# A four-layer graph network on gathered neighbours: scores one block ahead of the products, and a norm split over two engines, in layers two and three

## The chip, the cores and the metric

The kernel runs on one core of a Trainium2 chip. The metric is the device time of one execution in microseconds (us), lower is better; a version is stood for by the median of its runs. Five engines with queues of their own work side by side and wait for each other by semaphores: TensorE (PE; PEld is its weight load), VectorE (DVE), ScalarE (ACT), GpSimd (POOL) and SyncE (SP, which only issues transfers here).

## The reference

A graph of 4096 nodes with 256 features each goes through four pre-norm layers. Every layer is `x = x + attention(relu(layernorm(x)), adj)`, and they differ in the attention:

- layers one and three: four heads, score of an edge = leaky ReLU of a term of the node plus a term of its neighbour, softmax over the neighbours, weighted sum of the neighbours' projected rows (layer one has an ELU behind it);
- layer two: the same with one head; the projected row is added, and the unprojected rows are summed;
- layer four: four heads, score = q times k, softmax, weighted sum of v.

The adjacency is drawn with about eight edges to a node, besides a self loop, so a node has at most 23 neighbours here.

## The kernel before

**Tiling.** The nodes are sorted by their number of neighbours and cut into 32 blocks of 128, one node to a partition. `CAPS[b]` is the largest number of neighbours in block b, from 23 down to 3. A layer is 32 steps, one block to a step, in the order `ORDER`: 0, 30, 1, 29, 2, 28 and so on, and last 14, 16, 15, 31. In the code the four layers are l = 0 to 3; layers two and three are l = 1 and l = 2. The stages of the program one after the other: the scan of the adjacency (0 to some 371 us, with part of layer one in it), the rest of layer one (`late`), then `layer(1)`, `layer(2)` and `layer(3)`.

**Rows by gather.** Every layer reads the rows of its neighbours from a table in DRAM that the layer before wrote. One neighbour slot of one block is one indirect DMA of 128 rows, issued by POOL (`fetch`, L1030) into a ring of slots in SBUF: 270 gathers to a layer (a block's own cap, 15 at most, and one for the nodes with more). `fill(i)` puts the gathers of up to four blocks ahead of step i into POOL's queue; the first gather of a block waits for the last product of the blocks that had its slots (L1357). A layer's first gather waits for the whole table.

**A step of layers two and three.** For block b = `ORDER[i]`:

- `scores` (L1495): ACT (l = 1) or DVE (l = 2) adds the neighbours' terms, which waits for the block's gathers; for l = 1 DVE also compares lists (`mutual`, L1564 and L1568, which read the gathers too); DVE takes leaky ReLU and maximum (L1522, L1548 or L1552), ACT the exponential (L1550 or L1556).
- `weigh` (L1571): DVE normalises the shares (L1582 to L1584), multiplies the block's own row (L1595) and the gathered rows (L1610), and PE sums the rows into a PSUM bank (L1590, L1617, L1623). I call these the products of the block.
- `settle` (L1630): DVE adds up the sum into x (L1644) and takes mean and variance (`normed`, L955 and L957); ACT makes scale and bias of it in eight small instructions (L960 to L967).
- `norm`: ACT applies norm and ReLU (L970), PE transposes (L980). `flip`: ACT copies the transposed block to SBUF (L982).
- `product`: PE multiplies with the next layer's weights (L1023). `third`: DVE or ACT moves the result out of PSUM (l = 1: L1663 or L1665; l = 2: four instructions of DVE, L1683 to L1694, and ACT's squares, L1697), and SP writes it to the next layer's table (L1667, L1685). I call this the row of the block.

**Order.** PE, DVE, ACT and SP run their instructions in the order in which the code emits them, and in layers two and three POOL too. The stages of older blocks stand in a step at fixed lags: with `left` steps to go, `settle` is S blocks behind, `norm` N, `flip` F, `product` Q and `third` T. Far from the end these are 2, 3, 4, 5 and 6, and at the end 1, 2, 2, 2 and 3. A step emits `norm`, `product`, `scores`, `weigh`, `settle`, `flip`, `third`. There are four PSUM banks for the transposes and the rows; when none is free, `room` emits older `flip` and `third` stages early. A stage that reads a bank in a later step than the one that filled it waits for the last product of the step that filled it (`told_by`, L1385). PSUM also holds the shares, in two halves that the blocks take in turn (`self.turns`).

Of the kernel before, what the change touches and what calls it, by code (L numbers as in the profile page):

```python
# [9 lines left out]
F32 = mybir.dt.float32  # L10
# [9 lines left out]
P = 128  # L20
D = 256
# [52 lines left out]
RAW = 6  # L74

AHEAD = 4

BOUND = 4900.0


class Sparse:
# [869 lines left out]
    def normed(self, pool, xt, name):  # L951

        nc, act = self.nc, self.nc.scalar.activation
        st = pool.tile([P, 6], F32, name=f"s_st_{name}", tag="st", bufs=3)
        nc.vector.bn_stats(st, xt)  # L955
        mv = pool.tile([P, 2], F32, name=f"s_mv_{name}", tag="mv1", bufs=3)
        nc.vector.bn_aggr(mv, st)  # L957
        y = pool.tile([P, 6], F32, name=f"s_y_{name}", tag="y1", bufs=3)
        log, root, less, minus, r, at = (y[:, k : k + 1] for k in range(6))
        act(log, mv[:, 1:2], AF.Ln, bias=self.eps)  # L960
        act(less, mv[:, 1:2], AF.Identity, bias=self.minus, scale=-0.5)
        act(root, log, AF.Exp, scale=-0.5)
        act(minus, mv[:, 0:1], AF.Copy, scale=-1.0)
        act(log, root, AF.Square)
        act(less, less, AF.Identity, bias=self.three, scale=log)
        act(r, less, AF.Copy, scale=root)
        act(at, minus, AF.Copy, scale=r)  # L967
        yield None
        h = pool.tile([P, D], F32, name=f"s_h_{name}", tag="h", bufs=2)
        act(h, xt, AF.Relu, bias=at, scale=r)  # L970
        yield h

# [337 lines left out]
    def layer(self, l):  # L1310


        nc, nt, vs = self.nc, self.nt, {}
# [65 lines left out]
                held[j] = (s, s + room)  # L1379
                at = s + room if K else at  # L1380

        sums, behind, turning, flipped, rows = {}, {}, {}, {}, {}
        self.spot, signals, when = None, {}, {}

        def told_by(i, others, step):  # L1385
# [11 lines left out]
        def settle(c):  # L1397
            behind[c] = self.settle(l, c, sums.pop(c), made)
            for _ in range(2):
                next(behind[c])  # L1400

        def room(k):
            if len(self.free) < k:
                upto("flip", done["norm"] - 1)
                upto("third", done["product"] - 1)

        def norm(d):
            if l < 3:
                room(1)
                turning[d] = self.turned(self.pool, next(behind.pop(d)), f"{l + 1}_{d}")  # L1410
                next(turning[d])
                when["turn", d] = now, self.wrote

# [29 lines left out]
                self.tc.declare_no_dep(i, group="results", reason="places differ")  # L1443
                self.tc.add_to_no_dep_group("results", i)

        stages = {"settle": settle, "norm": norm, "flip": flip, "product": product, "third": third}
        done = {name: 0 for name in stages}

        def upto(name, k):
            while done[name] <= k:  # L1450
                stages[name](ORDER[done[name]])
                done[name] += 1

        for i in range(nt):
            now = i
            left = nt - 1 - i
            if l == 3:
                S = 1 if left < 3 else 2
                N = F = Q = S + 1
                T = N  # L1460
            else:
                S = 1 if left < 5 else 2
                N = 2 if left < 4 else 3
                Q = 2 if left < 2 else 3 if left < 4 else 4 if left < 6 else 5
                F, T = max(N, Q - 1), Q + 1
            fill(i)
            if (l, i) == (2, 4):
                self.symmetric()
            b = ORDER[i]
            upto("norm", i - N)  # L1470
            upto("product", i - Q)
            g = ring[:, held[b][0] : held[b][1], :]
            p = self.scores(l, b, self.rows[b], g)
            if l == 3:
                upto("third", i - T)
            sums[b] = self.weigh(l, b, vs.pop(b) if l == 3 else self.rows[b][:, 0:D], g, p)
            start, end = held.pop(b)
            past.append((start * wide, end * wide, self.read))
            if l < 3:
                signals[i] = self.read[1]  # L1480
            upto("settle", i - S)
            if l < 3:
                upto("flip", i - F)
                upto("third", i - T)
        now = nt
        upto("norm", nt - 2)
        upto("third", nt - 3)
        upto("product", nt - 2)
        upto("settle", nt - 1)
        upto("norm", nt - 1)  # L1490
        upto("third", nt - 2)
        upto("product", nt - 1)
# [2 lines left out]
    def scores(self, l, b, mine, g):  # L1495

        nc, pool = self.nc, self.pool
        H = 1 if l == 1 else 4
        G = self.slots(l, b)
        K = CAPS[b]  # L1500
        more = b == 0
        e = pool.tile([P, TOPK, H], F32, name=f"s_e_{l}_{b}", tag="e", bufs=3)
        ek = e[:, : K + 1, :].rearrange("p k h -> p (k h)")
        if l < 3:
            src = mine[:, D + H : D + 2 * H]
            if l == 1:
                nc.scalar.activation(e[:, :G, 0], g[:, :G, D], AF.Identity, bias=src)
                nc.scalar.activation(e[:, K, :], mine[:, D : D + H], AF.Identity, bias=src)
            else:
                first = nc.vector.tensor_tensor(e[:, K, :], mine[:, D : D + H], src, ALU.add)  # L1510
                nc.vector.tensor_tensor(
                    e[:, :G, :], g[:, :G, D : D + H],
                    src.unsqueeze(1).to_broadcast([P, G, H]), ALU.add,
                )
            if l == 1:
                self.mutual(b, g)

                nc.scalar.copy(self.near[:, b, 0:G], g[:, :G, WL - 1])
            if more:
                self.more_scores(l, mine, g[:, KEPT, :], e)  # L1520
            slope = 0.01 if l == 1 else 0.2
            steep = nc.vector.scalar_tensor_tensor(ek, ek, slope, ek, ALU.mult, ALU.max)  # L1522
            if l == 2:
                self.tc.declare_no_dep(steep.ins, first.ins, reason="another sum comes after it")
        else:
            q = self.shares[:, IB - D :]
            nc.scalar.copy(q, mine[:, 0:D])
            nc.scalar.copy(e[:, K, :], self.eself[:, b, :])
            for k0 in range(0, G, AT_ONCE):
                m = min(AT_ONCE, G - k0)  # L1530
                kq = g[:, k0 : k0 + m, 0:D]
                nc.vector.tensor_tensor(  # L1532
                    kq, kq, q.unsqueeze(1).to_broadcast([P, m, D]), ALU.mult
                )
                nc.vector.tensor_reduce(  # L1535
                    e[:, k0 : k0 + m, :], kq.rearrange("p k (h d) -> p k h d", h=4), AX.X, ALU.add
                )
            nc.vector.tensor_tensor(
                e[:, :G, :], e[:, :G, :],
                self.away[:, b, :G].unsqueeze(2).to_broadcast([P, G, 4]), ALU.add,  # L1540
            )
            if more:
                self.more_scores(l, mine, g[:, KEPT, :], e)
        by_head = e[:, : K + 1, :].rearrange("p k h -> p h k")
        top = pool.tile([P, H], F32, name=f"s_m_{l}_{b}", tag="m", bufs=3)
        p = self.shares[:, ts(self.turns % 2, TOPK * H)].rearrange("p (k h) -> p k h", h=H)
        if l == 1:
            nc.vector.tensor_reduce(top, by_head, AX.X, ALU.max, negate=True)  # L1548
            tot = pool.tile([P, H], F32, name=f"s_t_{l}_{b}", tag="t", bufs=3)
            nc.scalar.activation(ek, ek, AF.Exp, bias=top, accum_out=tot)  # L1550
            return e, p, tot
        nc.vector.tensor_reduce(top, by_head, AX.X, ALU.max)  # L1552
        nc.vector.tensor_tensor(  # L1553
            by_head, by_head, top.unsqueeze(2).to_broadcast([P, H, K + 1]), ALU.subtract
        )
        nc.scalar.activation(p[:, : K + 1, :].rearrange("p k h -> p (k h)"), ek, AF.Exp)  # L1556
        return p, p, None
# [13 lines left out]
    def weigh(self, l, b, me, g, made):  # L1571
# [12 lines left out]
        nc.vector.tensor_tensor(  # L1584
            whole(p), whole(exps), tot.unsqueeze(2).to_broadcast([P, H, K + 1]), ALU.mult
        )
        self.turns += 1
        v0 = 0 if l < 3 else D
        acc = self.pacc.tile([P, 2, D], F32, tag="acc", name=f"s_acc_{l}_{b}")
        self.took_x[b] = nc.tensor.matmul(  # L1590
# [39 lines left out]
    def settle(self, l, b, acc, made):  # L1630


        nc, pool = self.nc, self.pool
        xt = self.x[b]
        yield None
        if l == 3:
            tag = ("out", "kv")[ORDER.index(b) % 2]
            wide_as = 2 * D if tag == "kv" else D
            y = pool.tile([P, wide_as], F32, name=f"s_out_{b}", tag=tag, bufs=3)[:, 0:D]
            nc.vector.tensor_reduce(y, acc.rearrange("p u d -> p d u"), AX.X, ALU.add)  # L1640
            made.append((self.out, self.own(b), y))
            yield None
            return
        s = nc.vector.tensor_reduce(xt, acc.rearrange("p u d -> p d u"), AX.X, ALU.add)  # L1644
        self.tc.declare_no_dep(
            s.ins, self.took_x.pop(b).ins, reason="the sum's last product comes after it"
        )
        yield from self.normed(pool, xt, f"{l + 1}_{b}")
# [627 lines left out]
```

## Time and profile before

| | |
|---|---|
| runs shown | median 1672.91 us of 9 (1669.1 to 1674.16) |
| the profiled execution | 1673.22 us, its span 1671.5 us |
| busy share of the span | POOL 68%, DVE 66%, PE 65%, ACT 32% |
| mean granted clock of PE | 0.829 |
| layer two's gathers | 542.8 to 880.1 us |
| layer three's gathers | 906.6 to 1244.7 us |
| layer four's gathers and sends | 1279.4 us to the end |

The profile is of one execution. Its busy shares count work alone: POOL's queue also spends some time between two gathers that is not counted. Times of rows below count from the start of the span; the execution is 1.7 us longer than its span.

### The profile page before, as it was taken

To read this page: it belongs to the slowest core of one execution; us is meant where nothing else is said; L and a number is where in the kernel's file an instruction comes from. 1 tells how busy PE (TensorE), PEld (TensorE's weight loads), DVE (VectorE), ACT (ScalarE), POOL (GpSimd) and SP (SyncE) were. 2 spreads that over 40 slices of the span, in tenths; PEclk is the share of its full clock that TensorE was granted. 3 is DMA by queue.
4 is the path that set the end of the run, shared out by engine and by line. 5 is a ranking of instruction groups with operands and counts; after the bars stand their busy time and mean duration, and the time that the engine had idled before them with its cause. 6 is when DMAs were issued, how large, how long until landed. Compare 5 with 4: busy or idle time off the path is not lost.

```text
span 1671.5 us, 14539 instructions
## 1 busy us (share of the span) xinstructions
PE 1081.1 (65%) x3166; PEld 588.0 (35%) x3179; DVE 1109.2 (66%) x2651; ACT 536.1 (32%) x1754; POOL 1140.9 (68%) x1241
## 2 busy tenths in 40 slices
PE   5858888705776357777784467878794464645455
PEld 4423333204443134444342234444452232322232
DVE  6669899816885255455552456766774797888786
ACT  6866664003344033343343023333342000000000
POOL 1267777767774777777772777777752777777775
PEclk9969989856897678898897689999997677777877
DMA  7899999476551444444452435444443776767674
GB/s 271 299 396 394 358 395 325 143 230 161 156 164 64 116 118 129 131 132 132 130 140 63 109 108 145 137 134 139 141 127 97 216 220 205 213 206 211 205 206 130
DMA packets 125910, 309.11 MB, mean 185 GB/s; under 512 B 35028, under 2 KB 53463, under 8 KB 125816
## 3 DMA queue, kind: packets, MB, share of 16 engines
q0 software_dynamic: 66832, 203.64, 41.6%
q1 hardware_dynamic: 58984, 104.46, 17.6%
q8 instruction: 29, 0.48, 0.1%
q14 instruction: 65, 0.53, 0.1%
HBM read 273.00 MB, written 35.00 MB: 184 GB/s over the span
## 4 chain that ended last, share of the span: by engine, by line
POOL 26%; DMA 23%; DVE 20%; issue 16%; ACT 9%; PE 5%; DVEq 0%; SPq 0%; POOLq 0%; ACTq 0%
POOL s_ring L1030 22%; DMA s_ring<-s_tab,s_near 11%; DMA s_raw<-in_adj_dram 11%; DVE s_ring L1610 5%; DVE s_ring L1532 2%; ACT s_low L277 2%; DVE s_e L1535 2%; POOL s_placed L721 2%; PE s_bank L1023 1%; DVE s_rx L1644 1%; DVE s_me L1595 1%; POOL s_g L1030 1%; PE s_acc L1617 1%; PE s_ps_t L1023 1%; POOL out_dram L1047 1%
## 5 line engine op out<-in xcount | busy, mean ns | idle before, releaser
L1030 POOL DMA_INDIRECT s_ring<-s_tab,s_near x900 | 854.4, 949 | 338.0 <-issue 262.7
L1617 PE MATMUL s_acc<-s_ring,s_ident 128*128 128x512 f32 (+1 forms) x1002 | 467.1, 624 | 276.6 <-DVE s_ring L1610 276.4
L1617 PEld LDWEIGHTS s_acc<-s_ring,s_ident 128*128 128x128 f32 x1002 | 226.5, 233 | 494.8 <-DVE s_ring L1610 305.8
L1030 POOL DMA_INDIRECT s_g<-s_tab,s_keep x192 | 182.8, 952 | 129.6 <-DMA s_raw<-in_adj_dram 65.1
L1610 DVE TENSOR_TENSOR s_ring<-s_ring,s_shares 128x2048 f32<-128x2048 f32 (+1 forms) x153 | 233.0, 1553 | 0.0
L277 ACT ACTIVATE s_low<-s_raw 128x1024 fp8e4<-128x1024 int32 x128 | 135.1, 1056 | 61.2 <-DMA s_raw<-in_adj_dram 59.6
L1556 ACT ACTIVATE s_shares<-s_e 128x40 f32<-128x40 f32 (+7 forms) x64 | 13.1, 205 | 329.6 <-DVE s_e L1553 329.6
L520 PE MATMUL s_pt<-s_low,s_mark_True 128*128 128x512 fp8e4 x256 | 83.5, 406 | 53.0 <-DVE s_cand L532 45.3
L1532 DVE TENSOR_TENSOR s_ring<-s_ring,s_shares 128x2048 f32<-128x2048 f32 (+7 forms) x47 | 78.8, 1676 | 55.0 <-DMA s_ring<-s_tab,s_near 36.9
L960 ACT ACTIVATE s_y<-s_mv,s_eps 128x1 f32<-128x1 f32 x64 | 18.8, 294 | 276.6 <-DVE s_mv L957 250.5
L532 DVE MAX8 s_cand<-s_pt 128x8 f32<-128x256 f32 x256 | 93.3, 418 | 13.8 <-PE s_pt L530 12.2
L1564 DVE TENSOR_SCALAR s_eq<-s_ring,s_own_f 128x207 bf16<-128x207 f32 (+12 forms) x32 | 12.5, 390 | 129.5 <-DMA s_ring<-s_tab,s_near 129.1
L630 PE MATMUL s_ae<-s_g,s_ident 128*128 128x512 f32 x192 | 95.1, 626 | 3.7 <-DVE s_g L621 3.5
L1535 DVE TENSOR_REDUCE s_e<-s_ring 128x32 f32<-128x2048 f32 (+7 forms) x47 | 78.9, 1679 | 1.6
L1023 PE MATMUL s_bank<-s_wkv,s_ht 128*128 128x512 f32 x128 | 62.9, 615 | 3.6 <-ACT s_ht L982 3.6
L1023 PE MATMUL s_ps<-s_we_l,s_ht 128*128 128x264 f32 x128 | 45.9, 514 | 23.9 <-ACT s_ht L1271 23.9
L520 PEld LDWEIGHTS <-s_mark_True 128*128 128x128 bf16 x256 | 23.4, 100 | 104.2 <-issue 56.6
L1590 PE MATMUL s_acc<-s_rx,s_ident 128*128 128x256 f32 x192 | 59.4, 392 | 0.0
L1623 PE MATMUL s_acc<-s_me,s_ident 128*128 128x256 f32 x192 | 57.5, 381 | 0.0
L1268 PE MATMUL s_pht<-s_ident,s_rx 128*128 128x128 f32 x64 | 13.9, 330 | 65.6 <-DMA s_ring<-s_tab,s_near 47.7
L621 DVE TENSOR_TENSOR s_g<-s_g,s_pe 128x1536 f32<-128x1536 f32 x32 | 55.4, 1738 | 0.0
L922 PE MATMUL s_bank<-s_to,s_to_row 128*128 128x32 f32 (+1 forms) x6 | 1.8, 394 | 81.0 <-DVE s_to L916 81.0
(286 smaller groups left out, 1828.9 us busy)
## 6 DMA issues: line engine op xcount, KB each, us to landing
s_raw<-in_adj_dram SPq DMA_DIRECT2D x128, 512.0 KB, 9.7
s_ring<-s_tab,s_near POOLq DMA_INDIRECT x900, 3.0
s_rx<-s_placed SPq DMA_DIRECT2D x32, 262.0 KB, 3.2
s_tab<-s_kv SPq DMA_DIRECT2D x32, 256.0 KB, 2.3
s_tab<-s_rx SPq DMA_DIRECT2D x32, 132.0 KB, 1.9
s_keep<-in_x_dram SPq DMA_DIRECT2D x8, 512.0 KB, 9.0
s_vself<-s_tab SPq DMA_DIRECT2D x32, 128.0 KB, 3.4
s_tab<-s_keep SPq DMA_DIRECT2D x7, 528.0 KB, 4.1
```

The source lines that it names most:

```text
L277: nc.scalar.activation(low[r][:, quarter(q)], raw.pop(q), AF.Copy, saturate=False, accum_out=self.sums[:, r, h : h + 1],)
L520: nc.tensor.matmul(pt, lhsT=self.mark[k], rhs=lo[:, k * PAIR + g * IB : k * PAIR + (g + 1) * IB], start=(k == 0), stop=False,)
L532: nc.vector.max(out=cand[:, g * (IB // CH) + k, :], in_=pt[:, ts(k, CH)])
L630: nc.tensor.matmul(acc, lhsT=self.ident, rhs=g[:, :, k, 0:D], start=False, stop=(k == E - 1))
L1023: self.writes(self.nc.tensor.matmul(ps[:, :width], lhsT=ht[:, c, :], rhs=w[:, c, :], start=(c == 0 and bias is None), stop=(c == KC - 1),))
L1030: return self.nc.gpsimd.indirect_dma_start(out=out, out_offset=None, in_=table[:, :], in_offset=bass.IndirectOffsetOnAxis(ap=idx, axis=0),)
L1532: nc.vector.tensor_tensor(kq, kq, q.unsqueeze(1).to_broadcast([P, m, D]), ALU.mult)
L1535: nc.vector.tensor_reduce(e[:, k0 : k0 + m, :], kq.rearrange("p k (h d) -> p k h d", h=4), AX.X, ALU.add)
L1590: self.took_x[b] = nc.tensor.matmul(acc[:, 1, :], lhsT=self.ident, rhs=self.x[b], start=True, stop=False)
L1610: nc.vector.tensor_tensor(v, v, p[:, k0 : k0 + m, :].unsqueeze(3).to_broadcast([P, m, H, D // H]), ALU.mult)
L1617: nc.tensor.matmul(acc[:, 0:n, :], lhsT=self.ident, rhs=g[:, k : k + n, v0 : v0 + D], start=False, stop=False,).ins
L1623: last = nc.tensor.matmul(acc[:, 0, :], lhsT=self.ident, rhs=mev, start=False, stop=True).ins
```

## The change

It has three parts, all in layers two and three.

1. `scores` of block i + 1 is emitted in step i, ahead of `weigh` of block i, as long as more than one step is left. The last block's scores stay in their own step. The count that chooses the half of the shares moves from `weigh` to `scores`.
2. ACT's part of the norm (the eight small instructions and the ReLU) leaves `settle` and `norm` and becomes a stage of its own, `curve`, Y blocks behind. `norm` keeps the transposes.
3. The lags become a table by the steps left. Far from the end `settle`, `curve`, `norm`, `flip`, `product` are 2, 3, 4, 5, 6 blocks behind, and `third` is one more than `product`. Within a step `score`, `norm` and `product` now stand in this order.

The tile of the normed block has three buffers instead of two, and layer four's result tile shares them.

```diff
+LAGS = [
+    (1, 1, 2, 2, 2), (1, 1, 2, 2, 2), (1, 1, 2, 2, 3), (1, 1, 3, 3, 3), (1, 2, 3, 3, 4),
+    (2, 2, 3, 3, 4), (2, 2, 4, 4, 5), (2, 3, 4, 5, 6),
+]
...
         log, root, less, minus, r, at = (y[:, k : k + 1] for k in range(6))
+        yield None
         act(log, mv[:, 1:2], AF.Ln, bias=self.eps)
...
-        h = pool.tile([P, D], F32, name=f"s_h_{name}", tag="h", bufs=2)
+        h = pool.tile([P, D], F32, name=f"s_h_{name}", tag="h", bufs=3)
...
+        def curve(c):
+            if l < 3:
+                next(behind[c])
+                bent[c] = next(behind.pop(c))
...
-                turning[d] = self.turned(self.pool, next(behind.pop(d)), f"{l + 1}_{d}")
+                turning[d] = self.turned(self.pool, bent.pop(d), f"{l + 1}_{d}")
...
+        def score(i):
+            b = ORDER[i]
+            if b not in scored:
+                scored[b] = self.scores(l, b, self.rows[b], block(b))
...
-            else:
-                S = 1 if left < 5 else 2
-                N = 2 if left < 4 else 3
-                Q = 2 if left < 2 else 3 if left < 4 else 4 if left < 6 else 5
-                F, T = max(N, Q - 1), Q + 1
...
+            else:
+                S, Y, N, F, Q = LAGS[min(left, len(LAGS) - 1)]
+                score(i)
+                if left > 1:
+                    score(i + 1)
+                upto("norm", i - N)
+                upto("product", i - Q)
+                sums[b] = self.weigh(l, b, self.rows[b][:, 0:D], block(b), scored.pop(b))
+                signals[i] = self.read[1]
...
             upto("settle", i - S)
             if l < 3:
+                upto("curve", i - Y)
                 upto("flip", i - F)
-                upto("third", i - T)
+                upto("third", i - Q - 1)
...
         upto("settle", nt - 1)
+        upto("curve", nt - 1)
         upto("norm", nt - 1)
...
-            tag = ("out", "kv")[ORDER.index(b) % 2]
+            tag = ("h", "kv")[ORDER.index(b) % 2]
```

More of the change, by code (lines that the diff above doesn't have):

```diff
@@ L1380, in fill @@
                 at = s + room if K else at
-        sums, behind, turning, flipped, rows = {}, {}, {}, {}, {}
+        sums, behind, bent, turning, flipped, rows = {}, {}, {}, {}, {}, {}
         self.spot, signals, when = None, {}, {}
@@ L1444, in third @@
                 self.tc.add_to_no_dep_group("results", i)
-        stages = {"settle": settle, "norm": norm, "flip": flip, "product": product, "third": third}
+        stages = {
+            "settle": settle, "curve": curve, "norm": norm, "flip": flip, "product": product,
+            "third": third,
+        }
         done = {name: 0 for name in stages}
@@ L1452, in upto @@
                 done[name] += 1
+        block = lambda b: ring[:, held[b][0] : held[b][1], :]
+        scored = {}
+        def score(i):
+            b = ORDER[i]
+            if b not in scored:
+                scored[b] = self.scores(l, b, self.rows[b], block(b))
         for i in range(nt):
@@ L1456, in layer @@
             left = nt - 1 - i
[L1457 to L1460, printed above, removed]
-            else:
-                S = 1 if left < 5 else 2
-                N = 2 if left < 4 else 3
-                Q = 2 if left < 2 else 3 if left < 4 else 4 if left < 6 else 5
-                F, T = max(N, Q - 1), Q + 1
             fill(i)
@@ L1469, in layer @@
             b = ORDER[i]
[L1470 to L1473, printed above, removed]
             if l == 3:
-                upto("third", i - T)
-            sums[b] = self.weigh(l, b, vs.pop(b) if l == 3 else self.rows[b][:, 0:D], g, p)
+                S = 1 if left < 3 else 2
+                score(i)
+                upto("third", i - S - 1)
+                sums[b] = self.weigh(l, b, vs.pop(b), block(b), scored.pop(b))
+            else:
+                S, Y, N, F, Q = LAGS[min(left, len(LAGS) - 1)]
+                score(i)
+                if left > 1:
[4 more added lines that the diff above has]
+                signals[i] = self.read[1]
             start, end = held.pop(b)
             past.append((start * wide, end * wide, self.read))
-            if l < 3:
-                signals[i] = self.read[1]
             upto("settle", i - S)
             if l < 3:
+                upto("curve", i - Y)
                 upto("flip", i - F)
-                upto("third", i - T)
+                upto("third", i - Q - 1)
         now = nt
@@ L1546, in scores @@
         p = self.shares[:, ts(self.turns % 2, TOPK * H)].rearrange("p (k h) -> p k h", h=H)
+        self.turns += 1
         if l == 1:
@@ L1586, in weigh @@
         )
-        self.turns += 1
         v0 = 0 if l < 3 else D
```

## The prediction

> **What bounds the kernel now.** I read the page's chain that ended last first: POOL's gathers (L1030) lead it with 22%, and "issue" has 16%. So I cut the span where POOL's queue pauses and asked for the busy times of the stretches: layer two's gathers, the pause behind them, layer three's gathers, the pause behind those. The columns are PE, PEld, DVE, ACT and POOL busy (with instructions), PE's clock, DMA share and GB/s.
>
> ```profile
> 542.80:880.10 337.30, 231.82 (x666) 130.18 (x666) 163.12 (x353) 110.18 (x469) 255.26 (x270) 0.83 0.47 128
> 880.10:906.60 26.50, 17.87 (x57) 11.27 (x56) 10.59 (x30) 10.76 (x44) 0.01 (x1) 0.82 0.13 44
> 906.60:1244.70 338.10, 244.35 (x719) 136.54 (x720) 216.35 (x519) 105.59 (x424) 256.09 (x270) 0.88 0.47 130
> 1244.70:1279.40 34.70, 26.16 (x75) 13.88 (x73) 21.12 (x58) 15.00 (x59) 0.04 (x1) 0.90 0.14 51
> ```
>
> The reader is to see that 270 gathers take 337.3 and 338.1 us, 1.25 us each, in both layers, though DVE has 163 us of work in one and 216 us in the other. What they wait for, by the groups of POOL from 600 to 1278 us:
>
> ```profile
> L1030 POOL DMA_INDIRECT s_ring<-s_tab,s_near x494 | 467.8, 947 | 176.7 <-issue 161.5 <-DVE s_shares L1584 1.8 <-DVE s_ring L1610 1.5
> ```
>
> A gather is busy 947 ns and then idles some 0.30 us in "issue", with no engine to blame. The layers run at POOL's pace from the first gather to the last. What an order of DVE, ACT and PE can win or lose is then **the two pauses, 26.5 and 34.7 us**: the time from the last gather until the last block's row is in the next table. So I read DVE in time around their starts. The end of layer two:
>
> ```profile
> 871.90 0.16 DVE L1583 RECIPROCAL s_t<-s_t 128x1 f32<-128x1 f32 x1 [0.52 <-ACT s_e L1550]
> ...
> 872.64 2.28 DVE L1610 TENSOR_TENSOR s_ring<-s_ring,s_shares 128x2048 f32<-128x2048 f32 x1
> 874.84 0.68 DVE L1644 TENSOR_REDUCE s_rx<-s_acc 128x256 f32<-128x512 f32 x1
> ...
> 876.02 0.18 DVE L957 BATCH_NORM_AGGREGATE s_mv<-s_st 128x2 f32<-128x6 f32 x1
> 878.29 0.32 DVE L1564 TENSOR_SCALAR s_eq<-s_ring,s_own_f 128x184 bf16<-128x184 f32 x1 [2.08 <-DMA s_ring<-s_tab,s_near]
> ...
> 880.51 0.17 DVE L1522 SCALAR_TENSOR_TENSOR s_e<-s_e 128x9 f32<-128x9 f32 x1 [1.52 <-ACT s_e L1508]
> ...
> 881.39 0.16 DVE L1583 RECIPROCAL s_t<-s_t 128x1 f32<-128x1 f32 x1 [0.52 <-ACT s_e L1550]
> ...
> 890.16 0.16 DVE L1522 SCALAR_TENSOR_TENSOR s_e<-s_e 128x4 f32<-128x4 f32 x1 [3.79 <-ACT s_e L1508]
> ```
>
> Here 871.90 to 876.2 is block 16, the third from the end: its products, then the `settle` of block 14. Only then does DVE wait, 2.08 us, for the gathers of block 15 (878.29). **DVE spends the wait for the next block's gathers on this block's products.** The end of layer three:
>
> ```profile
> 1235.89 0.20 DVE L1582 TENSOR_REDUCE s_t<-s_shares 128x4 f32<-128x36 f32 x1 [0.71 <-ACT s_shares L1556]
> ...
> 1239.11 0.68 DVE L1644 TENSOR_REDUCE s_rx<-s_acc 128x256 f32<-128x512 f32 x1
> ...
> 1240.38 0.66 DVE L1683 TENSOR_TENSOR s_kv<-s_bank,s_bqkv 128x512 f32<-128x512 f32 x1
> ...
> 1243.42 0.69 DVE L1683 TENSOR_TENSOR s_kv<-s_bank,s_bqkv 128x512 f32<-128x512 f32 x1 [1.13 <-PE s_acc L1623]
> ...
> 1250.12 0.20 DVE L1582 TENSOR_REDUCE s_t<-s_shares 128x4 f32<-128x36 f32 x1 [0.27 <-ACT s_shares L1556]
> ```
>
> Block 16's products begin at 1235.89, `settle` of block 14 follows at 1239.11, three rows (L1683 to L1694, the first at 1240.38) come next, and block 15's products begin at 1250.12. Its last gather's data arrived at about 1242.8: DVE and PE are behind here.
>
> **The change, part by part.** No instruction and no transfer is added or removed; the order of four queues changes. POOL's queue keeps its order.
>
> *While POOL gathers: nothing.* ACT's and DVE's waits for each other get shorter, but a gather starts 1.25 us after the last one whatever they do. The cover is POOL's queue. It would be gone if a gather had to wait for its slots, since the products now come up to a block later. Layer two's first reuse of slots is block 3's gather at 614.12, over those of block 0, whose products left DVE at 574.4: some 40 us of room, against one block's gathers of at most 20 us. Price: 0.
>
> *Scores ahead, at the end of layer two.* Block 15's scores now stand ahead of block 16's products in DVE's queue, and their first instruction waits for data that is released at about 878.2. Behind it stand the products of block 16 and `settle` of block 14, and behind these PE's sums, the rows and the last two blocks. DVE: 878.29, plus the scores (0.7 for L1564 and L1568, 0.4 for L1522 and L1548), is 879.4; block 16's products, 871.90 to 874.92, are 3.0, to 882.4; `settle`, 1.36, to 883.8. Block 15's products begin there instead of at 881.39: +2.3 us on DVE, in which the 1.52 and 0.52 us waits for ACT are already gone. PE: block 16's sum takes 4.1 us (874.98 to 879.11), from 882.4 to 886.5; the transposes and two rows that follow it, 3.7 (879.21 to 882.93), to 890.2; block 15's sum, 4.3, to 894.5; the next transposes and row, 1.9, to 896.4; block 31's ten matmuls at 0.215, 2.2, to 898.6. Before, that sum ended at 894.9. So PE is what is late next: **+3.6**, which the last block's norm, row and write pass on. Bounds: 0, if ACT's wait of 3.79 us at 890.16 took up the delay (it can't well, since what ACT is busy with there follows block 16's `settle`, which is late itself), and +5 with PE at a lower clock.
>
> *Scores ahead, at the end of layer three.* Block 15's scores can run at 1242.8 and take 1.2 us (1248.86 to 1250.1): 1244.0. Then block 16's products, 3.2, one row, 1.9, `settle` of block 14, 1.3: 1250.4. The second row was filled by PE in block 16's step, so it waits for that step's last sum (the 1.13 us row at 1243.42 is such a wait); PE needs 4.2 us for it behind DVE's products, which end at 1250.1 if the first row goes ahead: 1254.3. Two rows of 1.9 with 0.3 between them: 1258.4. Block 15's products begin there instead of at 1250.12, **+8.3**, and the same instructions as before follow. Bounds: +4.0, if DVE never waited for PE (1242.8 + 1.2 + 3.2 + 1.3 + 3 x 1.87 = 1254.1), and +12 with PE at a lower clock.
>
> *ACT's part of the norm later.* Far from the end it is hidden by POOL. At the end the table sets Y to S from four steps before the last on, so the last norms follow at once, as before: 0. The larger lags (third 7 instead of 6 blocks behind) leave one row more to be caught up in the last eight steps, 1.9 us of DVE and 2.6 of PE in layer three; by the last three steps both tables have the same rows left, so I add nothing.
>
> *The shares' halves.* In the trace ACT's L1527, which writes another part of the shares' bank, waits 2.11 us until DVE's L1610 of block 31 ends at 1260.46. So parts of that bank are not free of each other, and block i's products in layer three may wait for block i + 1's exponential: 0 to 0.5 us (the 0.27 and 0.71 us rows of L1582). I take 0.
>
> *PE's clock.* The profile grants PE 0.50 at 890.0 to 893.4, 900.3 to 906.6, 1258.7 to 1262.1 and 1268.9 to 1272.3, and about 1.0 between. I leave those as they are; my bounds hold one such stretch of 3.4 us more in each pause (1.7 us each), or one less. [...]
>
> **Sum.** 3.6 + 8.3 = 11.9 us on the profiled execution's 1673.2: 1685.1. That execution is 0.3 us above the median of the runs shown, 1672.9; I predict 1685.
>
> **The rivals.** (1) *Faster:* the waits of DVE for ACT are what makes the pauses long, and with them go PE's idle stretches. [...] For it: 3.79 and 2.80 us of DVE waiting for ACT in the pauses. Against it: those two belong to block 31, whose scores are not moved. It decides if block 15's products begin earlier than before: less than 5.5 us after the last gather in layer three. 12%. (2) *No change:* the delay is taken up by waits that are there anyway, or the queues keep their order: 1670 to 1676. Against it: DVE and PE are behind at the end of layer three. 10%. (3) *Slower, as summed:* 75%. (4) *Much slower:* the steps themselves become DVE's and PE's, so that gathers wait for slots. It decides where 40 us of room are used up; at 0.5 us a step over 64 steps, +32: 1705. Against it: 216 us of DVE work in 338. 3%.
>
> **The numbers.** The likeliest case gives 1685, by its bounds 1677 (0 + 4.0) to 1690 (5 + 12). To leave out no more than 2 in 10, the range reaches over "no change" and a little above: 1670 to 1691. A measurement of this kernel can tell about 0.2%, 3.3 us, from no change. Faster 0.12, same 0.10, slower 0.78.
>
> **What would show it.** Right: the gathers of each layer still take 337 to 338 us; the pauses are some 30 and 43 us; DVE's wait for block 15's gathers stands ahead of block 16's L1583 or L1582, and these begin 7 to 11 us later against POOL's last gather than they did. Wrong: pauses as long as before or shorter, block 15's products at the old distance from the last gather, or POOL idle between gathers.

## The result, and the profile after

The changed kernel takes **1684.86 us** (median of 10 runs, 1683.38 to 1686.89); the kernel before, run beside it, 1673.55 us (median of 30). The ratio is **1.007**, with a 95% interval of 1.0061 to 1.008. The profiled execution took 1686.1 us, with a span of 1684.1 us.

The lines of the code stand five lower around the gathers (L1030 is L1035) and about twenty lower around the scores (L1522 is L1541, L1564 is L1584, L1582 to L1584 are L1602 to L1604, L1610 is L1629, L1623 is L1642, L1644 is L1663, L1683 is L1702). I cut the span where POOL pauses, as before; the columns are PE, PEld, DVE, ACT and POOL busy, PE's clock, DMA share and GB/s.

```profile
542.60:879.96 337.36, 227.79 (x644) 128.21 (x644) 155.78 (x351) 108.74 (x461) 255.41 (x270) 0.82 0.46 128
879.96:908.97 29.01, 22.09 (x78) 14.25 (x78) 13.85 (x33) 13.70 (x52) 0.01 (x1) 0.90 0.12 39
908.97:1247.15 338.18, 238.22 (x682) 134.10 (x683) 207.79 (x507) 101.26 (x404) 256.25 (x270) 0.86 0.46 129
1247.15:1292.86 45.71, 36.30 (x112) 20.53 (x110) 28.00 (x69) 20.80 (x80) 0.00 (x0) 0.93 0.12 44
```

The gathers take as long as before. The pauses grew from 26.54 to 29.01 and from 34.74 to 45.71 us: 2.47 + 10.97 = 13.4. The span is 12.6 longer, since layer four's part is 0.9 shorter in this execution. The second pause holds more work as well: PE 112 matmuls instead of 75, DVE 69 instructions instead of 58. What used to be done while the last gathers were on their way now stands behind them. The gathers' group from 600 to 1290 us says that no gather waited for a slot:

```profile
L1035 POOL DMA_INDIRECT s_ring<-s_tab,s_near x493 | 467.1, 947 | 178.9 <-issue 165.2 <-DMA s_ring<-s_tab,s_near 1.5 <-DVE s_eq L1584 1.2
```

DVE in time at the end of layer two:

```profile
878.30 0.48 DVE L1584 TENSOR_SCALAR s_eq<-s_ring,s_own_f 128x184 bf16<-128x184 f32 x1 [4.58 <-DMA s_ring<-s_tab,s_near]
...
879.35 0.15 DVE L1603 RECIPROCAL s_t<-s_t 128x1 f32<-128x1 f32 x1
...
883.57 0.13 DVE L1603 RECIPROCAL s_t<-s_t 128x1 f32<-128x1 f32 x1
...
891.53 0.16 DVE L1541 SCALAR_TENSOR_TENSOR s_e<-s_e 128x4 f32<-128x4 f32 x1 [3.03 <-ACT s_e L1527]
...
898.67 0.69 DVE L1663 TENSOR_REDUCE s_rx<-s_acc 128x256 f32<-128x512 f32 x1 [2.73 <-PE s_acc L1642]
```

The wait for block 15's gathers is 4.58 us instead of 2.08, and block 16's products (the first L1603) stand behind it, at 879.35; they had left DVE by 874.9. The wait for the gathers is no longer filled. The last line, 898.67, is the last block's sum, and it waits for PE. Layer three, first DVE's last wait for gathers, then its end:

```profile
1205.17 0.20 DVE L1530 TENSOR_TENSOR s_e<-s_ring,s_rx 128x36 f32<-128x36 f32 x1 [2.91 <-DMA s_ring<-s_tab,s_near]
...
1241.61 0.19 DVE L1602 TENSOR_REDUCE s_t<-s_shares 128x4 f32<-128x40 f32 x1
...
1246.44 0.13 DVE L1529 TENSOR_TENSOR s_e<-s_rx 128x4 f32<-128x4 f32 x1
...
1249.57 0.69 DVE L1702 TENSOR_TENSOR s_kv<-s_bank,s_bqkv 128x512 f32<-128x512 f32 x1 [1.93 <-PE s_acc L1642]
...
1251.42 0.18 DVE L1602 TENSOR_REDUCE s_t<-s_shares 128x4 f32<-128x36 f32 x1
...
1258.99 0.69 DVE L1702 TENSOR_TENSOR s_kv<-s_bank,s_bqkv 128x512 f32<-128x512 f32 x1 [3.01 <-PE s_acc L1642]
...
1263.40 0.18 DVE L1602 TENSOR_REDUCE s_t<-s_shares 128x4 f32<-128x36 f32 x1
```

The three L1602 are the first instructions of the products of blocks 14, 16 and 15. The last gather ended at 1247.15: block 15's products begin 16.25 us behind it, where they began 5.49 us behind it before (1250.12 against 1244.63). That is +10.8, almost the whole of the pause's +11.0. Two of the rows between them wait for PE, 1.93 and 3.01 us. None of them waits for gathers, as DVE is behind here: in the kernel before, block 16's products left DVE 5.4 us ahead of the end of the last gather (1239.19 against 1244.63); in the changed kernel they begin 4.3 us behind it (1251.42 against 1247.15). The layer ends about one block's work further behind.

### The profile page after: what moved, and what is told of

Same layout as the page of the kernel before. It is cut to its first block, busy times and chain, and to the rows that moved or that the text cites. A ratio compares the mean times of both kernels' runs of the same rounds, so it can differ in the third digit from the quotient of the medians.

```text
span 1684.1 us, 14541 instructions
## 1 busy us (share of the span) xinstructions
PE 1081.8 (64%) x3166; PEld 592.7 (35%) x3179; DVE 1103.7 (66%) x2651; ACT 538.9 (32%) x1754; POOL 1141.4 (68%) x1241
## 5 line engine op out<-in xcount | busy, mean ns | idle before, releaser
L1035 POOL DMA_INDIRECT s_ring<-s_tab,s_near x900 | 854.8, 950 | 353.1 <-issue 272.2
L1035 POOL DMA_INDIRECT s_g<-s_tab,s_keep x192 | 182.7, 951 | 131.3 <-DMA s_raw<-in_adj_dram 67.6
L1629 DVE TENSOR_TENSOR s_ring<-s_ring,s_shares 128x2048 f32<-128x2048 f32 (+1 forms) x153 | 233.0, 1553 | 0.0
L1584 DVE TENSOR_SCALAR s_eq<-s_ring,s_own_f 128x207 bf16<-128x207 f32 (+12 forms) x32 | 12.5, 392 | 178.9 <-DMA s_ring<-s_tab,s_near 178.9
L524 PE MATMUL s_pt<-s_low,s_mark_True 128*128 128x512 fp8e4 x256 | 83.7, 407 | 55.6 <-DVE s_cand L536 47.4
L1530 DVE TENSOR_TENSOR s_e<-s_ring,s_rx 128x36 f32<-128x36 f32 (+12 forms) x32 | 6.2, 194 | 109.1 <-DMA s_ring<-s_tab,s_near 79.2
L1526 ACT ACTIVATE s_e<-s_ring,s_rx 128x9 f32<-128x9 f32 (+12 forms) x32 | 9.9, 308 | 200.4 <-DMA s_ring<-s_tab,s_near 193.4
L1642 PE MATMUL s_acc<-s_me,s_ident 128*128 128x256 f32 x192 | 59.6, 393 | 0.0
```

The source lines that it names most:

```text
L524: nc.tensor.matmul(pt, lhsT=self.mark[k], rhs=lo[:, k * PAIR + g * IB : k * PAIR + (g + 1) * IB], start=(k == 0), stop=False,)
L1035: return self.nc.gpsimd.indirect_dma_start(out=out, out_offset=None, in_=table[:, :], in_offset=bass.IndirectOffsetOnAxis(ap=idx, axis=0),)
L1629: nc.vector.tensor_tensor(v, v, p[:, k0 : k0 + m, :].unsqueeze(3).to_broadcast([P, m, H, D // H]), ALU.mult)
L1642: last = nc.tensor.matmul(acc[:, 0, :], lhsT=self.ident, rhs=mev, start=False, stop=True).ins
```

## The experiments

**Theory.** The gathers set the pace, so the change can only act in the two pauses; there the scores of block 15, standing in front of block 16's products, hold them until the last gathers have landed. **Rivals.** That ACT's later norm costs; that the scores cost wherever they are taken early; that the order of one layer moves the other layer's end.

The runs fall on four chips, and one number has to be known before any other. On one of the four the kernel before takes 1672.5 us, as in the result. On the other three it takes 1985, 1984 and 2005 us, the same kernel with the same instructions. So only runs of one chip are compared, and the two kinds of chip are told apart below. Each chip had its runs at one time only, so a chip and its moment can't be parted.

### Runs where the kernel before takes 1672.5 us

**The changed kernel again** (g1_changed; no edit).

> The changed kernel itself, unaltered, where the experiments run. Where the kernel before takes about 1985 us there: the variants with scores ahead took 0.991 to 0.995 of it, and this differs from the one with scores ahead in layer two alone (0.9947) only in layer three. Theory (the two pauses hold the whole cost, and gathers set the pace in between): ratio 1.004 to 1.007 there too. Rival (where the gathers no longer set the pace, scores ahead cover time that engines spend waiting for each other, and pay for the pauses): 0.990 to 0.998, with longer pauses than the kernel before all the same. Where the kernel before takes about 1673 us: 1685 again, 1.007.

1687.81 us (median of 4), ratio 1.0083 (1.0054 to 1.0112). The result repeats.

**The kernel before, for its trace** (g4_before; no edit).

> The kernel before, for its trace beside the others of this call. Theory: its first pause is 2 to 3 us shorter and its second 10 us or more shorter than those of the changed kernel, whatever the time of the whole is; rival: the pauses are the same within 2 us where the engines wait on something that the profile does not show.

1672.03 us. The pauses of these two, the kernel before first:

```profile
879.47:905.83 26.36, 17.69 (x56) 11.33 (x56) 10.58 (x30) 10.53 (x43) 0.00 (x1) 0.81 0.12 39
1244.18:1279.51 35.33, 26.21 (x83) 14.43 (x81) 22.23 (x60) 15.33 (x60) 0.01 (x1) 0.95 0.15 53
```

and the changed kernel:

```profile
881.24:910.24 29.00, 22.09 (x78) 14.20 (x78) 13.84 (x33) 13.71 (x52) 0.00 (x0) 0.90 0.12 40
1248.56:1294.19 45.63, 36.41 (x112) 20.39 (x110) 28.05 (x70) 20.88 (x81) 0.00 (x1) 0.92 0.12 44
```

Against the executions of the result the pauses repeat within 0.1 us (changed kernel) and 0.6 us (before): +2.6 and +10.3. Block 15's products begin 7.08 and 16.33 us behind layer three's last gather in these two, +9.3; the 5.49 us of the kernel before above is one execution's, and this one differs by 1.6 us.

**Each block's scores in their own step, the new lags kept** (g2_own_step).

```diff
                 score(i)
-                if left > 1:
-                    score(i + 1)
                 upto("norm", i - N)
```

> The changed kernel without scores ahead, with the new lags of ScalarE's norm. Where the kernel before takes about 1673 us, theory: 1670 to 1674, pauses of 26 and 34 us, that is the whole cost is that of the scores ahead. Rival (the later norm costs): 1678 or more. Where the kernel before takes about 1985 us: 0.997 to 1.000 of it, as twice before.

**1668.90 us, ratio 0.9975 (0.9961 to 0.9988).** A little below the range that the theory gave: the cost is that of the scores ahead, 18.9 us against the changed kernel, and what is left of the change *gains* 3.6 us. This version beats both kernels.

**Scores ahead in layer two alone** (g3_ahead_in_two).

```diff
-                if left > 1:
+                if left > 1 and l == 1:
                     score(i + 1)
```

> Scores ahead in layer two alone. Where the kernel before takes about 1673 us, theory: the first pause as in the changed kernel (29 us), the second as before (35 us): 1674 to 1677. Rival (layer two's order moves layer three's end as well): 1680 or more. Where the kernel before takes about 1985 us: 0.995.

1674.93 us, ratio 1.0014 (1.0001 to 1.0027), as the theory had it. The pauses of own step, then of ahead in two:

```profile
878.27:903.97 25.70, 17.18 (x50) 11.50 (x50) 10.02 (x27) 10.09 (x39) 0.00 (x1) 0.72 0.12 41
1241.78:1273.58 31.80, 24.06 (x82) 13.56 (x80) 21.37 (x55) 15.75 (x61) 0.01 (x2) 1.00 0.16 55
```

```profile
879.07:908.08 29.01, 22.09 (x78) 14.22 (x78) 13.85 (x33) 13.71 (x52) 0.01 (x1) 0.90 0.12 40
1246.50:1282.00 35.50, 27.60 (x83) 15.40 (x81) 21.37 (x55) 16.07 (x62) 0.00 (x1) 0.90 0.14 49
```

With scores ahead in layer two the first pause is that of the changed kernel to 0.01 us (29.01 and 29.00): that half of the change costs **3.3 us** there (29.01 - 25.70). That is net of PE's clock: own step's PE has 0.50 from 886.27 to 893.10, where ahead in two has 1.00 until 902.34, and the 14 matmuls from the row ahead of the last block's sum to the end of that sum take 6.86 us against 3.80. At one clock the order would cost some 6 us there, an estimate from these rows. Adding them in layer three takes the second pause from 35.50 to 45.63: **10.1 us**. Ahead in two and the changed kernel both have two stretches of 3.41 us at 0.50 in that pause, so this number is the order's; block 15's products begin 16.33 us behind the last gather instead of 6.03.

But the second pause of own step and of ahead in two, 31.80 and 35.50, has the same code in it, and DVE has 21.37 us of work in both. What differs is PE's clock, 1.00 and 0.90. Cut at the clock's own edges, ahead in two has two stretches of 3.41 us at 0.50:

```profile
1260.77:1264.18 3.41, 3.39 (x4) 1.51 (x5) 3.31 (x9) 1.40 (x8) 0.00 (x0) 0.50 0.00 0
...
1271.01:1274.42 3.41, 3.41 (x8) 1.92 (x7) 0.69 (x1) 2.12 (x9) 0.00 (x0) 0.50 0.02 6
```

and own step, at the same distances from its last gather, none:

```profile
1256.05:1259.46 3.41, 3.41 (x13) 2.28 (x12) 3.31 (x8) 1.73 (x9) 0.00 (x0) 1.00 0.00 0
...
1266.29:1269.70 3.41, 2.64 (x8) 1.34 (x9) 1.09 (x3) 1.50 (x6) 0.00 (x0) 1.00 0.21 77
```

In the first stretch PE gets through 4 matmuls in one kernel and 13 in the other. Half of 6.83 us is 3.4, and the pauses differ by 3.7. Against its last gather DVE is 0.36 us later in ahead in two ahead of the first stretch (block 31's products begin 13.44 and 13.08 us behind that gather) and 3.69 us later behind the second (the last row begins 31.92 and 28.23 us behind it). So the rival "layer two's order moves layer three's end" got some of its number (6.0 us between the two kernels instead of 3.3), by the clock and not by any wait in the code. Why the same code met the stretches in one kernel and not in the other isn't shown. In ahead in two PE was busy for 0.45 and 0.33 of the 3.41 us ahead of the two stretches; but in the result's trace of the kernel before it was busy for 0.46 of the time from 893.45 to 896.87, and had full clock (1.00) in the 3.41 us that follow.

### Runs where the kernel before takes 1984 to 2005 us

On the first such chip (before 1985.37 us), four kernels:

**Own step** (e1_own_step; the edit of g2_own_step): 1979.88 us, 0.9968 (0.9939 to 0.9996).

> The changed kernel without its scores ahead: every block's scores stand in their own step again; the table of lags and ScalarE's own stage stay. Theory H (held products: with the scores a block ahead, a block's products wait for the next block's gathers, and that lengthens the two pauses of the gathers from 26.5 and 34.7 us to 29.0 and 45.7): the pauses fall back to about 26 and 35 us, the time to about 1672 us (1669 to 1676), 0.993 of the changed kernel. Rival L (the larger lags leave more rows for the end of a layer): the pauses stay near 29 and 45, the time near 1685. Rival A (ScalarE's norm as a stage of its own costs): also near 1685.

**The lags of before, scores ahead kept** (e2_old_lags): 1973.76 us, 0.993 (0.9901 to 0.9959).

```diff
 LAGS = [
-    (1, 1, 2, 2, 2), (1, 1, 2, 2, 2), (1, 1, 2, 2, 3), (1, 1, 3, 3, 3), (1, 2, 3, 3, 4),
-    (2, 2, 3, 3, 4), (2, 2, 4, 4, 5), (2, 3, 4, 5, 6),
+    (1, 1, 2, 2, 2), (1, 1, 2, 2, 2), (1, 1, 2, 2, 3), (1, 1, 2, 2, 3), (1, 1, 3, 3, 4),
+    (2, 2, 3, 3, 4), (2, 2, 3, 4, 5), (2, 2, 3, 4, 5),
 ]
```

> The changed kernel with the lags of the kernel before in the table (ScalarE's stage as far behind as VectorE's part, as before); the scores stay a block ahead. Theory H: the pauses stay long, about 29 and 43 to 45 us, the time 1682 to 1685. Rival L: pauses of 26.5 and 35 us, 1673. The difference to the changed kernel is what the lags cost; H gives them 0 to 3 us, nearly all in layer three.

**Ahead in layer two alone** (e3_ahead_in_two; the edit of g3_ahead_in_two): 1973.32 us, 0.9947 (0.9923 to 0.997).

> The changed kernel with the scores ahead in layer two alone. Theory H: each layer's pause answers to its own order: layer two's pause stays at 29 us, layer three's falls to about 35; the time is 1675 us (1672 to 1678). A theory in which layer three's long pause comes from what layer two hands over, or from the lags, expects it to stay at 45, the time at 1685.

**Ahead, but not in the last ten steps** (e4_ahead_not_at_end): 1981.74 us, 0.9981 (0.9957 to 1.0005).

```diff
-                if left > 1:
+                if left > 10:
                     score(i + 1)
```

> The changed kernel with the scores ahead only while more than ten steps of a layer are left, then in their own step. Theory H (only the order at the end of a layer counts, since the gathers set the pace until then): pauses of about 26 and 35 us, the time 1672 us (1669 to 1676), as without any scores ahead. Rival B (the steps themselves fall behind all through the layer and the delay piles up): the pauses stay clearly above those of the kernel without scores ahead, the time at 1678 or more.

All four missed what was expected, which was for a chip like that of the result. On the second such chip (before 1983.66 us):

**Own step again** (f1_own_step): 1978.78 us, 0.9981 (0.9953 to 1.001).

> The kernel of e1 again, since on the chip of the first four runs even the kernel before took 1985 us and TensorE idled on its own issue, so that the gathers did not set the pace there. On a chip where the kernel before takes about 1673 us: theory H (with the scores a block ahead, products are held until the next block's gathers have landed, which lengthens the pauses between the layers' gathers from 26.5 and 34.7 us to 29.0 and 45.7) expects pauses of about 26 and 35 us and 1672 us (1669 to 1676). Rivals L (the larger lags) and A (ScalarE's norm as a stage of its own): 1683 to 1686. On a chip where the kernel before takes 1985 us again: 0.997 of it, as measured there.

**The old lags again** (f2_old_lags): 1964.84 us, 0.991 (0.9879 to 0.9941).

> The kernel of e2 again (scores ahead, the lags of the kernel before). Theory H: pauses of 29 and 43 to 45 us, 1682 to 1685 us. Rival L: pauses of 26.5 and 35 us, 1673 us. On a chip with 1985 us before: 0.993 of it.

**The last block's scores behind the products of the block before, old lags** (f3_last_scores; no other scores ahead): 1966.07 us, 0.990 (0.9863 to 0.9936).

```diff
             past.append((start * wide, end * wide, self.read))
+            if l < 3 and left == 1:
+                score(i + 1)
             upto("settle", i - S)
```

> The lags of the kernel before and ScalarE's part of the norm as its own stage, no scores ahead, except that the last block's scores stand right behind the products of the block before it, ahead of that step's settle and of ScalarE's eight small instructions. Theory H says that a block's scores gain where its gathers have landed already, as the last block's have: VectorE's wait of 3.79 us for ScalarE at the end of layer two and of 2.80 us at the end of layer three should go, the pauses be about 24 and 33 us, the time 1669 us (1665 to 1673). A theory in which any scores moved ahead hold back what stands behind them expects pauses of 26.5 and 35 us or more, 1674 us or more.

On the third (before 2004.51 us), **the same edit with the new lags** (h1_last_scores): 1989.45 us, 0.9935 (0.9907 to 0.9964).

> The new lags, each block's scores at its own step, but in layers two and three the last block's scores come right behind the products of the block before it, not in front of them. Theory (what costs is only that products stand behind the next block's scores, so early scores that hold back no products cost nothing): the first pause is 24 to 25 us where the kernel with own steps has 25.7, because ScalarE's answer to the last block's scores, for which VectorE waited 3.03 us there, comes under the sum of the block before; the second 29 to 35 us, by whether TensorE's half-clock stretches fall into it, as with own steps; where the kernel before takes about 1673 us, the time is 1665 to 1671. Rival (any score taken early costs, by ScalarE's or TensorE's part of it): 1675 or more. Where the kernel before takes about 1985 us: 0.990, as with the old lags.

What is different on these chips is seen best on one kernel, own step, by PE's group of the row sums there (f1_own_step):

```profile
L1634 PE MATMUL s_acc<-s_ring,s_ident 128*128 128x512 f32 (+1 forms) x1002 | 463.8, 610 | 309.5 <-issue 185.6 <-DVE s_ring L1627 89.2 <-DMA s_ring<-s_tab,s_near 34.5
```

and on the other kind of chip (g2_own_step):

```profile
L1634 PE MATMUL s_acc<-s_ring,s_ident 128*128 128x512 f32 (+1 forms) x1002 | 472.6, 631 | 297.1 <-DVE s_ring L1627 297.1
```

The ratios that were expected for such a chip came for own step and the old lags (0.997 and 0.993); that of the last scores with the new lags, 0.990, lies just outside its interval.

A matmul of this group is as long, 610 and 631 ns, but PE stands 185.6 us ahead of it "in issue", with no wait that the profile shows, where it stood none. That need not be PE's own: the trace of f1_own_step holds 8866 semaphore records and that of g2_own_step 28311, so most releasers can't be named there, and f1_own_step's profile page calls 16% of the chain that ended last "another core or an unknown queue". All engines stop at times: between 1379 and 1385 us, say, PE idles 1.19 and 1.03 us in issue, and ACT's and DVE's next instructions start together at 1384.54, after 6.77 and 4.86 us, with no engine named. A gather still follows the last one after 1.25 us, but eight or nine times a layer POOL idles 2 to 11 us before one, so layer two's 270 gathers take 382.8 us and layer three's 379.5, and the pauses of own step are 57.0 and 87.7 us. The condition on which the prediction stands, gathers that set the pace, doesn't hold there.

So these runs say little about the theory as it was put. Nor do the pauses follow it there. On the first of these chips they are 57.0 and 83.2 us with own step, 50.7 and 83.7 with scores ahead in layer two, where the theory has the first longer; 59.0 and 88.6 without scores ahead in the last ten steps, where it has both as with own step; and 58.6 and 92.4 with the old lags and scores ahead. These are single executions. The whole of e2_old_lags isn't slower than own step, and is below the kernel before. **Left open:** what holds the engines back on those chips; why variants with scores ahead are at or below the kernel before there; and whether the changed kernel would be too, since it was not run there, and no trace of the kernel before was taken there. What e2_old_lags, e4_ahead_not_at_end, f3_last_scores and h1_last_scores were to tell where the gathers set the pace was not measured: among others, if scores taken early but behind the products are free.

## Why the prediction was right, point by point

- **While POOL gathers, 0:** right. 337.36 and 338.18 us against 337.3 and 338.1, and no slots waited for.
- **Scores ahead, end of layer two, +3.6:** right in its chain, short in its last link. Block 15's products began at 883.57 against the last gather's end at 879.96, 3.61 us behind it instead of 1.34: +2.3, as predicted. The last block's sum reached DVE at 898.67, which is +3.8 by the same measure, against +3.6. What failed is "which the last block's norm, row and write pass on": before, ACT was still busy with the block before when the last block's statistics were ready, and began its eight small instructions 1.20 us behind them (897.55 against 896.35); now it begins them 0.03 us behind (900.07 against 900.04), and with PE's next transposes 1.3 of the 3.8 us come back. With own step as the base the term is 3.3, and some 6 at one clock; that 3.3 is near 3.6 is luck.
- **Scores ahead, end of layer three, +8.3:** right that the products come a block later and then wait for PE's sums, too small, and not by a wait for block 15's gathers, which DVE doesn't have at the end of this layer. Measured +11.0 in the result, 10.1 by ahead in two against the changed kernel. The sum has a slip of 1.0 us: 1244.0, a row of 1.9 and products of 3.2 give 1249.1 and not 1250.1, so its own terms make +7.3. Of the two waits for PE only the second was in it. In the trace the first row waits too (1.93 us at 1249.57), because block 14's products, themselves held, ended late on PE, and block 15's scores began at 1246.44, right behind them and 1.1 us later than in the sum. The second row then began at 1258.99; by the sum as it stands, set against the same last gather, it would have been 1256.8. That is 2.2 of the missing 2.5 us.
- **ACT's part of the norm later, 0:** wrong in size, and the step that failed is "the last norms follow at once, as before". The lags and the new order within a step, without scores ahead, gain 3.6 us in all (g2_own_step, 0.9961 to 0.9988). I read the table's lags and not what it does that `score` now stands in front of `norm` and `product`. In the kernel before, run with it, ACT first copied a block's transposes (L982), for which it waited for PE, and came to the last block's scores (L1507) then:

```profile
888.53 0.37 ACT L982 COPY s_ht<-s_bank 128x256 f32<-128x256 f32 x1 [0.53 <-PE s_bank L980]
888.80 0.30 ACT L1507 ACTIVATE s_e<-s_ring,s_rx 128x3 f32<-128x3 f32 x1
```

In own step the scores (L1524) go first, and the copy (L987) follows:

```profile
885.48 0.31 ACT L1524 ACTIVATE s_e<-s_ring,s_rx 128x3 f32<-128x3 f32 x1
...
886.75 0.35 ACT L987 COPY s_ht<-s_bank 128x256 f32<-128x256 f32 x1
```

  DVE's wait for these scores falls from 3.79 to 3.03 us, and its wait for the last block's shares in layer three from 2.79 to 1.88. In the pauses it is 0.7 and 3.5 us by these two traces; of the second, how much is the order and how much the clock (one stretch of 3.41 us at 0.50 in the kernel before, none in own step) can't be parted, since ahead in two has the same order there and no gain (35.50). No run has this order alone, so that it gains, and not the lags, is read from these rows.
- **PE's clock kept, 0:** right for the sum of the first pause, which was at full clock until 902.97; the stretch at 0.50 that began at 890.0 is gone from the trace (1.00 from 889.93 to 893.34). The sum of +3.6 has full clock from 890.2 to 893.4 too, where the kernel before had 0.50; no run shows what would lift that, and the changed kernel had 1.00 from 879.96 to 902.97. PE was busy for 0.56 of the 3.41 us ahead of 889.93 in the kernel before and for all of them in the changed kernel, but a cause isn't shown by that. The 1.7 us for a stretch more or less fit too (3.3 of 3.7 us for two), but two can come or go in one pause, where I allowed for one.
- **The shares' halves, 0:** nothing on the path waits for them: the L1602 of block 15 at 1263.40 has no wait.
- **The rivals.** *Faster* was to win by the waits of DVE for ACT. One of its parts is real, but belongs to the order within a step and not to the scores ahead. It was to be told by block 15's products less than 5.5 us behind the last gather, and they are 16.25 us behind it. *No change* and *much slower* are out by the pauses and by the gathers. Of the signs of being right, the first instruction of block 16's products was to come 7 to 11 us later against the last gather: it comes 7.5 us later in layer two and 13.0 in layer three.
- **The sum.** 11.9 predicted. The result's medians differ by 11.3, those of g1_changed and the kernel before beside it by 15.3. That 11.9 is so near 11.3 is in part luck: against the executions of the result the first term is 1.1 too large, the second 2.7 too small, layer four's part 0.9 shorter without a forecast, and the median of the changed kernel is 1.2 below its profiled execution. By the medians of g1 to g3: scores ahead in layer two +6.0 (3.3 in its pause, 3.7 in the other, 3.3 of it by the clock, the rest scatter), in layer three +12.9 (10.1 in its pause, 2.1 ahead of the first gather of layer two, where the two kernels have the same code, the rest scatter), the lags and the order -3.6.

## What to carry to other kernels

Where one engine's queue set the pace of a stage, here, a new order of the others acted only where that queue paused (13.4 us more in the two pauses, 337.36 and 338.18 us of gathers against 337.3 and 338.1); so cut the span at its pauses, and price the change there. An instruction that is moved up waits in its queue, in order, for the newest data (here 4.58 us instead of 2.08 for block 15's gathers): ask what stands behind it that was ready, and at the end of a stage try it behind that work, which was not measured where the gathers set the pace. Read the order of a step in full, since a part that was meant for something else (here `score` in front of `norm`) may be the one that gains.

## What the runs showed of the hardware that was not expected

- The same kernel, own step, takes 1669 us on one chip and 1979 to 1980 on two others. DVE, ACT and POOL are as long busy, within 8 us (1105.9, 532.0 and 1139.5 us against 1106.0, 539.1 and 1142.3), PE is 79 us longer (1157.2 against 1078.1, at a mean granted clock of 0.760 instead of 0.822), and the span is 307 us longer; the rest of that is idle time.
- PE's clock fell to 0.50 for stretches of 3.41 us, or more (6.3 us from 900.3 in the kernel before), in the pauses; PE was busy for 0.33 to 0.56 of the 3.41 us before them (by the modelled ends of its matmuls, in the result's traces of the two kernels). The same code met two such stretches in one kernel and none in another, beside a difference of 3.7 us.
